# Spreading the row-2 joining of a Winograd convolution over three steps of the vector engine's order

## The chip, the cores and the metric

The kernel runs on one core of one Trainium2 chip. The metric is the device time of one execution in microseconds; the runs shown for the kernel before are three, with a median of 3211.7 us (3210.56 to 3212.76). A profile is one more execution, recorded instruction by instruction. In it PE is the matrix engine, PEld its weight loads, DVE the vector engine, ACT the scalar engine, POOL and SP the other two; all five run their own instruction lists in order and wait for each other through semaphores.

## The reference

Four images of 256 channels and 64 x 64 points, in float32, pass four residual layers. Each layer is `x = x + layer(groupnorm(x))`.

```python
# layer 0: 3x3 convolution, group norm, relu, non-local attention over all 4096 points
xs = conv_general_dilated(x, smooth_w, (1, 1), 'SAME') + smooth_b
xs = relu(group_norm(xs, gn1_w, gn1_b))
f = einsum('bnc,bcm->bnm', theta_x, phi_x)      # theta, phi, g: 1x1 convolutions of xs, 128 channels
y = einsum('bnm,bmc->bnc', softmax(f), g_x)
layer0 = group_norm(conv1x1(y, w_w, w_b)) * 0.1 + xs
# layer 1: linear attention (4 heads of 32) between two rms norms
# layer 2: per-image 3x3 depthwise and 256x256 pointwise kernels, made from pooled features
# layer 3: a softmax mixture of four 256x256 matrices applied to every point
```

The change concerns the 3x3 convolution of layer 0 alone.

## The kernel before, in words

**Images and rounds.** The four images go one after another through layer 0's attention, which is PE's largest work. Image 0's convolution runs alone at the start (`convolve_first`). Then come rounds b = 0, 1, 2: while PE does the attention of image b (`attend`, line 604 on), the engines also do layers 1 to 3 of image b - 1 (`tail`; in round 0 only a weight scaling) and then the convolution of image b + 1 (`convolve`, line 472). A last round has no convolution.

**What sets the order.** The order on all engines is the order in which the Python code issues instructions (a manual schedule). The round's side work is a `Chain`, a generator that yields a cost in steps; a rate (1.5 in round 0, 0.86 in rounds 1 and 2) turns costs into steps of the attention. One attention step issues a block of logits (`pf`, line 620), its exponentials on ACT into `pr` (line 621), the products `py` of the block before (line 659) and DVE's addition of that block to the running sum `tot`. Between steps, `Chain.tick` runs what was put off by `w.later(n, f)`: f runs after n ticks.

**The convolution.** It is a Winograd scheme that makes 4 x 2 output points from tiles of 6 x 4 input points, 128 channels to a half, two halves. `a` counts the six input rows of a tile and `k` the four columns, in the order 1, 2, 0, 3. For each row a, DVE forms the row combination `ra` (with the helper `rt`) from the normalised image `xp` in `down` (line 329 on); these operations yield 0.35 each. Then for each k DVE forms `v` (`across`), and one tick later PE multiplies v with the filters `u` (`products`, line 377; four f32 products of 128 x 512, each two passes of PE, into two PSUM banks). For k = 1 ACT copies the banks to `one`; for the others DVE joins the banks one tick later into the row's result `dst` (`joined`, line 388).

**The joining of rows.** The results of rows 0, 1, 3 go directly into the output image `big`, at rows 0, 1, 3 of each group of four. Those of rows 2, 4, 5 go to a temporary `t` of the pool `k4` or are added. When row 2 is complete (k = 3), output rows 0, 1 and 2 are formed from it, for each of the two output halves `oh`, by the three operations of `joining` (line 426):

```python
return [(tt, y2, y1, t, ALU.add), (tt, y1, y1, t, ALU.subtract), (tt, y0, y0, y2, ALU.add)]
```

Each is one tensor_tensor of 128 x 1024 on DVE. In the kernel before, `join` puts both halves off by one tick, so all six stand together in DVE's list. Row 4, which has twelve such operations, goes another way: they are put in the list `rest`, and `some(3)` takes three of them at each of four ticks.

**Buffers.** `k4` holds ten tiles of 128 x 1024 that v, t, pr, tot and others share; `bank` holds PSUM's eight banks of 128 x 512, shared by all matrix products.

Of the kernel before, what the change touches and what calls it, by code (L numbers as in the profile page):

```python
# [14 lines left out]
NH = 2  # L15
# [66 lines left out]
def conv_preact_fast(ctx: ExitStack, tc: tile.TileContext, guard, x, wc, wtpg, ww, wqkv, wout, w1cat, wd2,  # L82
# [187 lines left out]
    def stats_tile():  # L270
        return sp.tile([P, NH, 8, 6], F32, name="st")
# [65 lines left out]
    def down(a, to, prior=None):  # L337

        A, T = inside(to), rt
        mul, add, sub = ALU.mult, ALU.add, ALU.subtract  # L340
        if a in (0, 5):
            lo = 0 if a == 0 else 1
            return [(stt, o, i, f, j, mul, add) for h in range(NH) for o, i, f, j in (
                (A[:, h], rows_of(lo + 2, h), -5.0, rows_of(lo + 4, h)), (A[:, h], rows_of(lo, h), 4.0, A[:, h]))]
        if a == 1:
            return [(stt, o[:, h], rows_of(k, h), -4.0, rows_of(k + 2, h), mul, add)
                    for h in range(NH) for o, k in ((A, 2), (T, 1))] + [(tt, A[:, h], A[:, h], T[:, h], add) for h in range(NH)]
        if a == 3:
            return [(tt, o[:, h], rows_of(k + 2, h), rows_of(k, h), sub) for h in range(NH) for o, k in ((A, 2), (T, 1))] + [
                (stt, A[:, h], T[:, h], 2.0, A[:, h], mul, add) for h in range(NH)]  # L350
        return [(stt, A[:, h], T[:, h], -2.0 if a == 2 else -4.0, inside(prior)[:, h], mul, add) for h in range(NH)]

    def across(k, rows):

        def col(j):
            return rows[:, :, :, j:j + MX * (IX - 1) + 1:MX]

        v = k4("v")
        first, second, op = ((0, 2, ALU.subtract), (1, 2, ALU.add), (2, 1, ALU.subtract), (1, 3, ALU.subtract))[k]
        tt(v.rearrange("p (h y x) -> p h y x", h=NH, x=IX), col(first), col(second), op)  # L360
        return v
# [78 lines left out]
    def input_stats():  # L440

        st = stats_tile()
        for h in range(NH):
            for c in range(8):
                nc.vector.bn_stats(st[:, h, c, :], xin[:, h, bass.ts(c, RB), :].rearrange("p y x -> p (y x)"))
                yield 0.3
        return (yield from group_finish(st, avg8, 1e-5))

    def normalise(gm, rstd):
        nb = negated(gm, rstd)  # L450
        for q in range(4):
            rows = bass.ts(q, HW // 4)
            nc.vector.tensor_scalar(xin[:, 0, rows, :], xin[:, 0, rows, :], gm[:, 0:1], rstd[:, 0:1],
                                    ALU.subtract, ALU.mult)
            nc.scalar.activation(xin[:, 1, rows, :], xin[:, 1, rows, :], AF.Identity,
                                 bias=nb[:, 1:2], scale=rstd[:, 1:2])
            yield 0.5

    def copy_x(b):
        for h in range(NH):  # L460
            nc.sync.dma_start(out=xs_d[b, h], in_=x[b, bass.ts(h, P), :])

    def normed_relu(w, b, st):

        bias = vec_s[:, V_SB, :]
        _, gm, rstd = yield from group_finish(st, avg32, 1e-5, bias)
        sc, sh = affine(gm, rstd, vec_s[:, V_G1W, :], vec_s[:, V_G1B, :], bias, 1.0)
        for c in range(N // CH):
            cols = bass.ts(c, CH)
            for h in range(NH):  # L470
                nc.scalar.activation(big[:, h, cols], big[:, h, cols], AF.Relu, bias=sh[:, h:h + 1], scale=sc[:, h:h + 1])  # L471
                w.later(1, lambda h=h, cols=cols: add_by_dma(xs_d[b, h, :, cols], big[:, h, cols]))
                yield 0.3

    def convolve(w, b):

        _, gm, rstd = yield from input_stats()
        yield from normalise(gm, rstd)
        st = stats_tile()
        products, joined, _, rows_joined, joining, stats = joiner(st)  # L480
        PRODUCTS = [(a, k) for a in range(TY) for k in ACROSS]

        rest = []

        def some(n):
            for _ in range(min(n, len(rest))):
                op, *args = rest.pop(0)
                op(*args)

        def multiply(a, k, v, u):  # L490
            ps = products(a, k, v, u)
            if k != 1:
                w.later(1, lambda: join(a, k, ps))

        def join(a, k, ps):
            dst = joined(a, k, ps)
            if k == 3 and a == 4:

                for oh in range(NH):
                    rest.extend(joining(a, oh, dst[oh]))  # L500
                for j in range(4):
                    w.later(1 + j, lambda: some(3))
                for j in range(3):
                    w.later(5 + j, lambda j=j: stats(j))
            elif k == 3:
                some(len(rest))
                for oh in range(NH):
                    w.later(1, lambda oh=oh: rows_joined(a, oh, dst[oh]))

        def load_filters(i):  # L510
            res = []
            for oh in range(NH):
                u = wk.tile([P, NH, P], F32, tag="u", name="u", bufs=4)
                nc.sync.dma_start(out=u, in_=filters[PRODUCTS[i][0], oh, :, PRODUCTS[i][1]])
                res.append(u)
            return lambda oh, h: res[oh][:, h, :]

        us = load_filters(0)
        copy_x(b)
        for i, (a, k) in enumerate(PRODUCTS):  # L520
            if k == 1:
                for op, *args in down(a, ra, ra):
                    op(*args)
                    yield 0.35
            v, u = across(k, ra), us
            if i + 1 < len(PRODUCTS):
                us = load_filters(i + 1)
            w.later(1, lambda a=a, k=k, v=v, u=u: multiply(a, k, v, u))
            yield 0.8
        yield from w.pending()  # L530
        stats(3)
        yield from normed_relu(w, b, st)
# [1196 lines left out]
```

## Time and profile before

| what | value |
|---|---|
| median of three runs | 3211.7 us |
| profiled execution, its own time | 3210.14 us |
| its span, first to last instruction | 3208.4 us |
| mean granted PE clock | 0.986 |
| PE busy | 3071.0 us (96%) |
| DVE busy | 2075.8 us (65%) |
| ACT busy | 1146.0 us (36%) |
| instructions | 24196 |
| DVE: row-2 and other additions of t into big, 128 x 1024 | 30, mean 1221 ns |
| DVE: v, 128 x 1024 | 72, mean 1220 ns |
| PE: 128 x 512 products of the convolution | 576 here, mean 599 ns |

Busy times overlap, and PE's matmuls are pipelined: a record of 592 ns starts about 430 ns after the one before. A wait row reads: who waited, for whom, us in total, times, longest. A timeline row reads: start, duration (of the group), engine, line, operation, output and inputs, shape, count, and in brackets the idle time ahead of it with its releaser. A row of the windows view has the stretch and its length, then for each engine the busy time and the number of instructions, then the PE clock granted, the share of the DMA engines and GB/s.

### The profile page before, as it was taken

The numbers are of one execution on the slowest core, as the hardware profiler recorded it, in microseconds if no ns is written. First come the engines' busy times: TensorE is split into PE (matmuls) and PEld (weight loads), VectorE is DVE, ScalarE is ACT, GpSimd is POOL, SyncE is SP. The second block draws the span as 40 slices with busy tenths as digits, with TensorE's granted clock in tenths as the row PEclk, the third lists the DMA queues.
The fourth block names the chain that finished last, engine by engine and source line by source line (L and its number), as shares of the span: only waits on it lengthen the run. The fifth ranks groups of instructions, "written<-read, shape, count | busy, mean of one in ns | idle before, by whom it ended". The sixth has DMA issues, their size and how long they took to land.

```text
span 3208.4 us, 24196 instructions
## 1 busy us (share of the span) xinstructions
PE 3071.0 (96%) x8494; PEld 1476.7 (46%) x8494; DVE 2075.8 (65%) x2603; ACT 1146.0 (36%) x2139; POOL 129.4 (4%) x169
## 2 busy tenths in 40 slices
PE   6899999999999999999999999999999999996797
PEld 3354444445564444444565444444555534443533
DVE  8636776443556986876537796878353768855575
ACT  2133224333555332223364432312355443333520
POOL 0000000000010000000011000000000100000100
PEclk9999999999999999999999999999999999998998
DMA  5510113001100023113200102210510010121101
GB/s 180 173 39 27 33 34 62 7 13 63 49 10 27 13 72 118 40 33 76 101 11 6 35 20 90 101 38 27 129 42 1 10 40 7 49 70 46 50 0 73
DMA packets 73792, 161.66 MB, mean 50 GB/s; under 512 B 7744, under 2 KB 39232, under 8 KB 70720
## 3 DMA queue, kind: packets, MB, share of 16 engines
q1 hardware_dynamic: 69056, 143.27, 13.1%
q0 software_dynamic: 4608, 16.78, 2.9%
q8 instruction: 69, 1.13, 0.2%
q14 instruction: 59, 0.48, 0.0%
HBM read 103.40 MB, written 73.40 MB: 55 GB/s over the span
## 4 chain that ended last, share of the span: by engine, by line
PE 79%; DVE 12%; issue 5%; ACT 2%; DMA 0%; POOL 0%; SPq 0%; POOLq 0%; ACTq 0%
PE pf L620 23%; PE py L659 23%; PE ps_conv L382 8%; PE ps_qkv L748 5%; DVE dw L112 4%; PE ps_tp L596 3%; PE ps_ex L1059 3%; PE ps_pw L922 2%; DVE tot L109 2%; PE ps_g L601 2%; PE ps_h L881 2%; PE ps_wy L643 2%; PE ps_o L813 1%; PE ps_ctx L768 1%; PE ps_ss L735 1%
## 5 line engine op out<-in xcount | busy, mean ns | idle before, releaser
L621 ACT ACTIVATE pr<-pf 128x512 f32<-128x512 f32 x1024 | 604.1, 596 | 1227.7 <-PE pf L620 1203.7
L620 PE MATMUL pf<-tpg 128*128 128x512 f32 x2048 | 968.7, 595 | 1.4 <-ACT pr L621 1.4
L659 PE MATMUL py<-pr,tpg 128*128 128x512 f32 x2048 | 962.1, 592 | 3.0 <-ACT pr L621 2.9
L109 DVE TENSOR_TENSOR tot<-tot,pr 128x1024 f32<-128x1024 f32 x448 | 546.5, 1220 | 263.3 <-ACT pr L621 261.7
L659 PEld LDWEIGHTS py<-pr,tpg 128*128 128x128 f32 x2048 | 388.8, 190 | 494.2 <-issue 478.3
L620 PEld LDWEIGHTS pf<-tpg 128*128 128x128 f32 x2048 | 381.6, 190 | 447.3 <-issue 419.2
L112 DVE SCALAR_TENSOR_TENSOR dw<-xp,dk,dw 128x1008 f32<-128x1008 f32 x224 | 283.1, 1268 | 7.0 <-ACT dw L914 3.7
L382 PE MATMUL ps_conv<-v,u 128*128 128x512 f32 x576 | 260.7, 599 | 12.7 <-issue 9.0
L382 PEld LDWEIGHTS ps_conv<-v,u 128*128 128x128 f32 x576 | 110.3, 192 | 154.0 <-issue 147.0
L748 PE MATMUL ps_qkv<-wqkv_s,xg 128*128 128x384 f32 x384 | 130.7, 490 | 0.0
L596 PE MATMUL ps_tp<-big,wtpg_s 128*128 128x512 f32 x256 | 116.8, 599 | 3.0 <-ACT big L471 3.0
L189 POOL TENSOR_TENSOR rstd<-rstd,half 128x2 f32<-128x2 f32 x24 | 16.8, 701 | 2478.8 <-DVE rstd L294 2285.2
L109 DVE TENSOR_TENSOR tpg<-ps_g,bg_s 128x512 f32<-128x512 f32 x32 | 22.1, 692 | 144.3 <-PE ps_g L601 144.3
L922 PE MATMUL ps_pw<-dw,pk 128*128 128x512 f32 x224 | 103.8, 597 | 10.9 <-DVE dw L112 10.9
L634 DVE RECIPROCAL inv<-pss 128x512 f32<-128x512 f32 x32 | 107.2, 3351 | 7.3 <-PE pss L632 7.3
L748 PEld LDWEIGHTS ps_qkv<-wqkv_s,xg 128*128 128x128 f32 x384 | 72.2, 190 | 52.5 <-issue 8.9
L756 DVE TENSOR_REDUCE qs<-qk 128x16 f32<-128x512 f32 x24 | 16.5, 686 | 123.4 <-ACT qk L750 123.4
L109 DVE TENSOR_TENSOR v<-ra 128x1024 f32<-128x1024 f32 x72 | 86.7, 1220 | 0.4
L597 ACT ACTIVATE tpg<-ps_tp,btp_s 128x512 f32<-128x512 f32 x64 | 43.7, 686 | 118.4 <-PE ps_tp L596 118.4
L922 PEld LDWEIGHTS ps_pw<-dw,pk 128*128 128x128 f32 x224 | 42.7, 191 | 65.4 <-issue 50.9
L596 PEld LDWEIGHTS ps_tp<-big,wtpg_s 128*128 128x128 f32 x256 | 47.5, 193 | 54.3 <-issue 49.8
L750 ACT ACTIVATE qk<-ps_qkv,rinv 128x256 f32<-128x256 f32 x96 | 45.4, 473 | 74.2 <-PE ps_qkv L748 71.2
(273 smaller groups left out, 2948.2 us busy)
## 6 DMA issues: line engine op xcount, KB each, us to landing
u<-filters SPq DMA_DIRECT2D x144, 128.0 KB, 2.3
xp<-in_x_dram SPq DMA_DIRECT2D x16, 1024.0 KB, 6.4
xs_d<-big POOLq DMA_DIRECT2D x32, 512.0 KB, 11.3
wy_d<-wt SPq DMA_DIRECT2D x32, 512.0 KB, 3.0
out_dram<-res SPq DMA_DIRECT2D x64, 256.0 KB, 2.0
wy<-wy_d SPq DMA_DIRECT2D x28, 512.0 KB, 5.1
xs<-xs_d SPq DMA_DIRECT2D x24, 512.0 KB, 5.3
wp<-in_wp_dram SPq DMA_DIRECT2D x16, 512.0 KB, 4.6
```

Source lines behind the costliest of these rows:

```text
L109: nc.vector.tensor_tensor(o, a, b, op)
L112: nc.vector.scalar_tensor_tensor(o, a, s, b, op0, op1)
L382: nc.tensor.matmul(ps[oh], u(oh, h), v[:, bass.ts(h, 512)], start=(h == 0), stop=(h == NH - 1))
L596: nc.tensor.matmul(ps, wtpg_s[:, h, k, :], big[:, h, cols], start=(h == 0), stop=(h == NH - 1))
L601: nc.tensor.matmul(ps[:, j, :], big[:, h, bass.ts(4 * c + j, P)], wtpg_s[:, h, 2, :], start=(h == 0), stop=(h == NH - 1))
L620: nc.tensor.matmul(pf, phi[:, bass.ts(2 * m + s, P)], theta[:, bass.ts(q, 512)], start=True, stop=True)
L621: nc.scalar.activation(pr[:, bass.ts(s, 512)], pf, AF.Exp)
L634: nc.vector.reciprocal(inv, pss)
L659: nc.tensor.matmul(py, g[:, bass.ts(2 * m + s, P)], probs[i][:, bass.ts(s, 512)], start=(m == 0 and s == 0), stop=(m == NM - 1 and s == 1))
L748: nc.tensor.matmul(ps[:, 0:3 * HID], xg[:, h, bass.ts(j, P)], wqkv_s[:, h, :], start=(h == 0), stop=(h == NH - 1))
L922: nc.tensor.matmul(ps, pk[:, h * NH * P + oh * P:h * NH * P + (oh + 1) * P], dw[h][:, bass.ts(s, 512)], start=(h == 0), stop=(h == NH - 1))
L1059: nc.tensor.matmul(ps, wm[h][:, bass.ts(oh, P)], big[:, h, cols], start=(h == 0), stop=(h == NH - 1))
```

## The change

In `join`, row 2 gets a case of its own. Its six operations go to the list `rest`, half 0's three first, and two of them are taken at each of the next three ticks. Rows 3 and 5 keep the old way, row 4 its own.

```diff
@@ -502,6 +502,11 @@
                     w.later(1 + j, lambda: some(3))
                 for j in range(3):
                     w.later(5 + j, lambda j=j: stats(j))
+            elif k == 3 and a == 2:
+                for oh in range(NH):
+                    rest.extend(joining(a, oh, dst[oh]))
+                for j in range(3):
+                    w.later(1 + j, lambda: some(2))
             elif k == 3:
                 some(len(rest))
                 for oh in range(NH):
```

`some(n)` takes up to n operations off the front of `rest` and issues them. In the built program the lists of PE, ACT, POOL and SP stand as before. On DVE the order changes at three places, one in each round with a convolution. With J1 to J6 for the six operations, ra and rt for row 3's input combination:

```
round 0 before: tot J1 J2 J3 J4 J5 J6 ra rt tot ra ra tot v tot v
round 0 after:  tot J1 J2 ra rt tot J3 J4 ra ra tot J5 J6 v tot v
rounds 1, 2 before: tot J1 J2 J3 J4 J5 J6 ra v tot v v tot v tot
rounds 1, 2 after:  tot J1 J2 ra v tot J3 J4 v v tot J5 J6 v tot
```

## The prediction

> **What bounds the kernel now.** I read the page's shares first, then its chain, then PE's waits, then the timeline of the one place that the diff touches.
>
> ```profile
> PE 3071.0 (96%) x8494; PEld 1476.7 (46%) x8494; DVE 2075.8 (65%) x2603; ACT 1146.0 (36%) x2139; POOL 129.4 (4%) x169
> PE 79%; DVE 12%; issue 5%; ACT 2%; DMA 0%; POOL 0%; SPq 0%; POOLq 0%; ACTq 0%
> PE ps_conv L382 <- issue: 9.0, 2, 4.5
> PE ps_conv L382 <- DVE v L109: 3.7, 2, 2.0
> ```
>
> PE is busy 96% of the span, so a DVE edit pays only where PE stands still for DVE. The last two lines (PE's waits) say that the convolution's products stood 9.0 us in two waits, longest 4.5, put down to "issue", and 3.7 us in two waits for v. The timeline of the round that convolves image 2 shows the first of the two 4.5:
>
> ```profile
> 1373.00 1.22 DVE L109 TENSOR_TENSOR tot<-tot,pr 128x1024 f32<-128x1024 f32 x1
> 1374.13 2.48 DVE L109 TENSOR_TENSOR big<-big,t 128x1024 f32<-128x1024 f32 x2
> 1376.53 1.22 DVE L109 TENSOR_TENSOR big<-big 128x1024 f32<-128x1024 f32 x1
> 1377.37 1.88 PE L659 MATMUL py<-pr,tpg 128*128 128x512 f32 x4
> 1377.66 2.48 DVE L109 TENSOR_TENSOR big<-big,t 128x1024 f32<-128x1024 f32 x2
> 1380.06 1.22 DVE L109 TENSOR_TENSOR big<-big 128x1024 f32<-128x1024 f32 x1
> 1381.19 1.22 DVE L112 SCALAR_TENSOR_TENSOR ra<-rt,ra 128x1024 f32<-128x1024 f32 x1
> 1382.44 1.23 DVE L109 TENSOR_TENSOR v<-ra 128x1024 f32<-128x1024 f32 x1
> 1383.77 5.37 PE L382 MATMUL ps_conv<-v,u 128*128 128x512 f32 x8 [4.52 <-issue]
> 1388.97 1.88 PE L620 MATMUL pf<-tpg 128*128 128x512 f32 x4
> ```
>
> The six joining operations of row 2 are the four DVE lines with big. Behind them stand row 3's last input operation (ra) and its first v; v ends at 1383.67 and the products start 0.10 later. So "issue" is this wait for v: it was held on a separate wait instruction in PE's queue, which this line of the products' source view shows as long as 8932 ns, from 1374.8 (hence to 1383.7):
>
> ```profile
> L382 PEldq EVENT_SEMAPHORE  x4: 51/51/8932, 1374.8 to 1391.5; - x4
> ```
>
> The eight matmuls then take 5.20 us to the next group, where the same eight take 3.43 later (1402.71 to 1406.14). The windows view has the clock: 0.90 over 17 us is half speed for 3.4 us.
>
> ```profile
> 1373.00:1390.00 17.00, 12.48 (x26) 5.24 (x25) 16.25 (x15) 3.56 (x6) 0.00 (x0) 0.90 0.02 8
> 2131.00:2148.00 17.00, 12.48 (x26) 5.12 (x25) 16.02 (x14) 3.75 (x7) 0.00 (x0) 0.90 0.02 8
> ```
>
> The round of image 3 is the same picture (second row): the joining at 2131.91, products at 2141.55 after 4.52 idle, next group 5.21 later. The round of image 1 is milder:
>
> ```profile
> 393.35 1.22 DVE L109 TENSOR_TENSOR v<-ra 128x1024 f32<-128x1024 f32 x1
> 394.62 3.70 PE L382 MATMUL ps_conv<-v,u 128*128 128x512 f32 x8 [2.03 <-DVE v L109]
> ```
>
> [...] both 4.52 us pauses were followed by 3.4 us at half, the 2.03 us one was not. [...] the trace has 1220, and independent ones start 1.13 apart. [...] here v waits behind the joining on DVE and PE's later groups behind the products.
>
> **The change part by part.** Nothing is added or removed: PE, ACT, POOL and SP keep their order, DMA issues included; on DVE six operations in each of three rounds move. Against the profiled execution (3210.14 us, span 3208.4):
>
> Round of image 2. New order: tot, J1, J2, ra, v, tot, J3, J4, v, v, tot, J5, J6, v. J1 starts at 1374.13 as before. The pair costs 2.40 (1374.13 to 1376.53), so ra starts at 1376.53, v 1.25 later (as 1381.19 to 1382.44) at 1377.78, ends at 1379.01, and PE may start at 1379.11. PE is free of its py group at 1377.37 + 4 x 0.43 = 1379.09. The products start at 1379.11 in place of 1383.77: 4.66. Without the pause I take the clock to stay full, 3.43 in place of 5.20: 1.77. Together 6.43.
>
> Round of image 3. J1 2131.91, ra 2134.31, v 2135.56 to 2136.79, products 2136.89 in place of 2141.55: 4.66; 5.21 becomes 3.43: 1.78. Together 6.44.
>
> Round of image 1. The chain ticks more often against the input operations, so all six still stand ahead of v: J1, J2, ra, rt, tot, J3, J4, ra, ra, tot, J5, J6, v. Before, the 12 operations from 379.47 took 13.88, with two pairs that cost 2.40 where free ones cost 2.27 (a wait for the operation just ahead). Now only the first pair pays it: v comes 0.13 earlier. The pause stays at 1.9.
>
> Sum 6.43 + 6.44 + 0.13 = 13.0: profiled time 3197.1. The runs shown have their median 1.6 above the profiled execution, at 3211.7; so 3198.7.
>
> **What the four deferred operations delay.** They cost nothing if DVE's later work still comes in time. For image 2, all of PE's times 6.43 earlier: after v, DVE runs tot 1378.92, J3 1380.05, J4 1381.19, v of k=2 1382.32 to 1383.55 (PE needs it at 1392.41 - 6.43 = 1385.98: 2.4 to spare, the narrowest), v of k=0 until 1384.7 (needed at 1389.4), tot, J5 1385.73, J6, v of k=3 1388.0 to 1389.2 (needed at 1396.28), tot, then the joining of k=2 from 1390.3 to 1392.7 and of k=0 to 1393.7. These free PSUM banks of the pool of 8: py, four for k=2 and k=0, two for logits make seven, k=3's first bank is the eighth, its second (1398.0) and the next logits (1406.14 - 6.43 = 1399.7) need freed ones: 5.3 and 6.0 to spare. Row 4's v, after two ra, ends at 1397.5 and is needed at 1403.15. The cover is DVE's idle time: 2.17 + 1.58 + 0.43 + 0.43 + 1.03 + 0.92 before 1407 on the old timeline, 6.6 us, which PE's new start eats. The tots, which free probabilities, come earlier (1378.92 for 1383.59, 1384.6 for 1386.99). Head 1's t stays in the k4 pool until J5, some 5 us longer; buffers rotate differently, and row 4's first v now also waits for a wy_d write, issued at 1321.53 with a median of 2.7 us to land: long done.
>
> **The rivals.** (1) The pause goes but the clock's half-speed stretches do not all: 13.0 less one or two of 1.77 is 9.5 to 11.2, so 3200.5 to 3202.2. For it: [...] the windows view has the clock at 0.99 between 780 and 935, though PE is busy 151.79 of those 155 us. Against: with v on time PE has no pause here. (2) PE stands for something other than v, and nothing changes: 3211.7. The word "issue" speaks for it; the 0.10 us from v's end in both rounds and the round of image 1, where the same wait is named v, speak against. (3) Partial debt: DVE is up to 3 us later than worked out, past the 2.4 us margin of v for k=2, and PE stops again there: 1 to 5 us back over two rounds, 3200 to 3204. (4) Slower: the same backlog decides at the PSUM banks. Each us that the joining of k=2 comes beyond the 5.3 us margin is a us of PE. To end 0.2% (6.4 us) above before, each round must give back 6.43 and lose 3.2 more, so the joining must come 15 us later than 1392.7, that is thirteen more 1.13 us operations ahead of it; only four are moved there. Time 3218 if it were so. I see no such work in the order.
>
> **How the numbers follow.** The main case has 0.76, with its own range 3196.5 to 3201.0: the runs shown spread by 2.2, and half-speed stretches elsewhere (the tail's clock is 0.92) may fall differently by one or two of 1.77. Rival 1 has 0.09, rival 3 0.06, rival 2 0.05, rival 4 0.04. The range 3195.5 (two such stretches fewer) to 3204.0 takes in the main case and rivals 1 and 3. A difference of 0.2% (6.4 us) is about what measurement can tell from none: main, rival 1 and most of 3 are faster, 0.90; same 0.06; slower 0.04.
>
> **What would show it.** In the changed kernel's PE waits, the "issue" row of ps_conv is gone or below 0.5 us and v's row stays near 3.6; the timeline has the products of row 3 in the second and third rounds start within 0.2 us of the py group's end, and the clock is 1.00 over those 17 us; the first round keeps a pause of about 1.9; DVE's busy time stays 2075.8 within 1. Wrong would be: a new wait of PE within 30 us after, on v or big, or the two pauses still there.

## The result, and the profile after

The changed kernel takes 3198.27 us (median of four runs, 3196.53 to 3198.95) against 3212.09 us for the kernel before (four runs, 3210.56 to 3212.76). The ratio is 0.9957, with a 95% interval of 0.994 to 0.9974. That is 13.8 us, where 13.0 was forecast; the time forecast was 3198.7. The profiled execution took 3198.95 us with a span of 3197.2, 11.2 less than before.

First the shares of the page, and three rows of PE's waits, of the changed kernel. Line numbers above 505 are five higher than before.

```profile
PE 3069.2 (96%) x8494; PEld 1476.0 (46%) x8494; DVE 2074.2 (65%) x2603; ACT 1146.1 (36%) x2139; POOL 129.2 (4%) x169
```

```profile
PE ps_row L414 <- DVE ra L112: 6.8, 1, 6.8
PE ps_conv L382 <- DVE v L109: 3.5, 2, 1.9
PE ps_tp L601 <- ACT big L471: 3.0, 1, 3.0
```

The work is the same: as many matmuls, as many DVE instructions. The row "ps_conv <- issue", 9.0 us in two waits, is gone, and the row for v is nearly what it was, 3.5 us for 3.7. The timeline of the round that convolves image 2 shows how:

```profile
1374.63 1.22 DVE L109 TENSOR_TENSOR tot<-tot,pr 128x1024 f32<-128x1024 f32 x1
1375.76 2.48 DVE L109 TENSOR_TENSOR big<-big,t 128x1024 f32<-128x1024 f32 x2
1378.15 1.22 DVE L112 SCALAR_TENSOR_TENSOR ra<-rt,ra 128x1024 f32<-128x1024 f32 x1
1378.99 1.88 PE L664 MATMUL py<-pr,tpg 128*128 128x512 f32 x4
1379.40 1.23 DVE L109 TENSOR_TENSOR v<-ra 128x1024 f32<-128x1024 f32 x1
1380.73 3.67 PE L382 MATMUL ps_conv<-v,u 128*128 128x512 f32 x8
1383.95 2.36 DVE L109 TENSOR_TENSOR v<-ra 128x1024 f32<-128x1024 f32 x2
1384.24 1.88 PE L625 MATMUL pf<-tpg 128*128 128x512 f32 x4
1387.67 7.03 PE L382 MATMUL ps_conv<-v,u 128*128 128x512 f32 x16
```

Two joining operations instead of six stand ahead of ra. v ends at 1380.63, and the products start at 1380.73, straight behind the py group (1378.99 + 4 x 0.43 = 1380.71). The products are four, and each shows as two matmul records. The next group follows 3.51 us later, not 5.20: the clock stayed at 1.00. The windows view says the same of both rounds (PEclk is the third number from the end):

```profile
1373.00:1390.00 17.00, 17.00 (x41) 7.50 (x40) 16.93 (x16) 4.76 (x8) 0.00 (x0) 1.00 0.05 15
2124.00:2142.00 18.00, 18.00 (x43) 7.81 (x42) 17.93 (x16) 5.04 (x9) 0.00 (x0) 1.00 0.06 16
```

PE is busy all of the 17 us, where it was busy 12.48 before. Measured from the tot ahead of the joining to the logits behind the first products, the round of image 2 took 15.97 before (1373.00 to 1388.97) and 9.61 now (1374.63 to 1384.24): 6.36 less. The round of image 3 went from 15.98 (2130.78 to 2146.76) to 9.62 (2125.98 to 2135.60): again 6.36. Both were forecast at 6.4. In the round of image 1 the pause stays, but in this execution the clock falls behind it, to 0.86 on the mean from 390 to 402 us, where it was 1.00 before:

```profile
392.50 1.88 PE L664 MATMUL py<-pr,tpg 128*128 128x512 f32 x4
396.28 5.40 PE L382 MATMUL ps_conv<-v,u 128*128 128x512 f32 x8 [1.90 <-DVE v L109]
401.51 1.02 PE L625 MATMUL pf<-tpg 128*128 128x512 f32 x2
```

The products to the next group take 5.23 us instead of 3.53 before.

### The profile page after: what moved, and what is told of

Read it like the earlier page. It is cut to its first block, busy times and chain, and to the rows that moved or that the text cites. A ratio compares the mean times of both kernels' runs of the same rounds, so it can differ in the third digit from the quotient of the medians.

```text
span 3197.2 us, 24194 instructions
## 1 busy us (share of the span) xinstructions
PE 3069.2 (96%) x8494; PEld 1476.0 (46%) x8494; DVE 2074.2 (65%) x2603; ACT 1146.1 (36%) x2139; POOL 129.2 (4%) x169
## 3 DMA queue, kind: packets, MB, share of 16 engines
q8 instruction: 69, 1.13, 0.2%
## 4 chain that ended last, share of the span: by engine, by line
PE 79%; DVE 12%; issue 5%; ACT 2%; DMA 0%; POOL 0%; SPq 0%; POOLq 0%; ACTq 0%
PE pf L625 23%; PE py L664 23%; PE ps_conv L382 8%; PE ps_qkv L753 5%; DVE dw L112 4%; PE ps_tp L601 4%; PE ps_ex L1064 3%; PE ps_pw L927 3%; DVE tot L109 2%; PE ps_g L606 2%; PE ps_h L886 2%; PE ps_wy L648 2%; PE ps_o L818 1%; PE ps_ctx L773 1%; PE ps_ss L740 1%
## 5 line engine op out<-in xcount | busy, mean ns | idle before, releaser
L820 ACT ACTIVATE junk<-ps_o 128x256 f32<-128x256 f32 x128 | 49.2, 384 | 63.5 <-PE ps_o L818 60.5
```

## The experiments

The theory was that a joining operation costs PE time only where it stands ahead of row 3's first v. Rivals: that taking two at a time is itself what helps; that the deferred work is paid for later; that DVE, at 65%, has room everywhere. In each group of runs the kernel before ran beside them on the same chip: 3211.09 us for the first four, 3211.19 for the others. The two agree within 0.1 us, so runs of both groups are set side by side.

**One round alone.** First the round of image 1 alone, then that of image 3 alone.

```diff
-            elif k == 3 and a == 2:
+            elif k == 3 and a == 2 and b == 1:
```

> The new place of the six operations in the round of image 1 alone; the rounds of images 2 and 3 as before. Theory (only operations that stand ahead of row 3's first v cost PE time): all six stay ahead of that v in this round, so PE's pause there goes from 2.03 to 1.9 us and the other two rounds keep 4.52 each; within 2 us of the kernel before. Rival (two at a time is itself what helps, wherever it is): a third of the gain, 4 us or more faster.

Measured: 3211.16 us, ratio 1.0 (0.9992 to 1.0009). The pause in that round is 1.90 us, the other two stay at 4.52:

```profile
PE ps_conv L382 <- issue: 9.0, 2, 4.5
...
PE ps_conv L382 <- DVE v L109: 3.6, 2, 1.9
```

Spreading the six operations in a round where they all stay ahead of v is worth nothing that can be measured. The rival of this run falls.

```diff
-            elif k == 3 and a == 2:
+            elif k == 3 and a == 2 and b == 3:
```

> The new place in the round of image 3 alone. Theory: that round's pause of 4.52 us and the half clock after it go, the others stay; 6.4 us faster than before (5 to 8.5). Rival (the gain comes from somewhere else, such as the other use of the buffers): not half of the whole change's gain.

Measured: 3204.21 us, ratio 0.9979 (0.9971 to 0.9986), so 6.9 us less: half of the change's gain. One of the two 4.52 us pauses is left, in the round of image 2, with half clock after it (5.21 us to the next group), and the round of image 3 shows none:

```profile
PE ps_conv L382 <- issue: 4.5, 1, 4.5
```

Image 2's round was not run alone. Twice 6.9 is 13.8 us, and the change gained 13.8 in its first measurement and 12.6 in its second, so the rounds add up as far as the scatter lets one see.

**How many stand ahead of v.**

```diff
-                    w.later(1 + j, lambda: some(2))
+                    w.later(1 + j, lambda n=(4, 1, 1)[j]: some(n))
```

> Four operations at the first step, then one and one: in the rounds of images 2 and 3 two more of the 1.13 us operations stand ahead of v than in the change. Theory: a pause of 2 x 1.13 = 2.3 us (2.0 to 2.4) in place of none in each of these two rounds, followed by half clock in some of them; 4.0 to 8 us slower than the change, still 5 to 9 us faster than before. Rival (spreading over steps is what helps): as fast as the change.

Measured: 3204.12 us, ratio 0.998 (0.9971 to 0.9988), so 5.5 us slower than the change (3198.61 in its second measurement, below). The timeline of the round of image 2:

```profile
1376.01 1.22 DVE L109 TENSOR_TENSOR big<-big 128x1024 f32<-128x1024 f32 x1
1377.15 1.22 DVE L109 TENSOR_TENSOR big<-big,t 128x1024 f32<-128x1024 f32 x1
1378.28 1.22 DVE L112 SCALAR_TENSOR_TENSOR ra<-rt,ra 128x1024 f32<-128x1024 f32 x1
1379.54 1.23 DVE L109 TENSOR_TENSOR v<-ra 128x1024 f32<-128x1024 f32 x1
```

```profile
1376.86 1.88 PE L664 MATMUL py<-pr,tpg 128*128 128x512 f32 x4
1380.87 3.67 PE L382 MATMUL ps_conv<-v,u 128*128 128x512 f32 x8 [2.13 <-issue]
```

The two added operations (the first two lines) hold v back, and PE pauses 2.13 us in both rounds. So six, four and two operations ahead give pauses of 4.52, 2.13 and none: 1.1 to 1.2 us for each, the time that it takes in DVE's order: in the trace of before, operations of this size last 1.22 us each, start 1.13 apart where they are independent, and a pair whose second waits for its first took 2.40. The two pauses are 4.3 of the 5.5 us. The work is spread over three steps here too, and that does not help.

**One lump, but behind v.** All six together, one tick later than before.

```diff
-                for j in range(3):
-                    w.later(1 + j, lambda: some(2))
+                for j in range(1):
+                    w.later(2, lambda: some(6))
```

> All six in one lump, as before, but one tick later than before, so in the rounds of images 2 and 3 they stand right behind row 3's first v and the addition after it; in the round of image 1 still ahead of v. Theory (position, not the spread, decides): no pause for this v in the two rounds; the lump ends just in time for the v of k=2, at most 0.3 us late; within 1.5 us of the change. Rival (the lump itself stops PE, wherever it is): pauses of 2 us or more at k=2, and the gain is half or less.

Measured: 3199.12 us, ratio 0.9963 (0.995 to 0.9977), the change's time within the scatter. The lump now stands between v and the two v of k = 2 and 0:

```profile
1376.10 1.23 DVE L109 TENSOR_TENSOR v<-ra 128x1024 f32<-128x1024 f32 x1
...
1378.37 2.48 DVE L109 TENSOR_TENSOR big<-big,t 128x1024 f32<-128x1024 f32 x2
1379.80 3.60 PE L382 MATMUL ps_conv<-v,u 128*128 128x512 f32 x8
1380.77 1.22 DVE L109 TENSOR_TENSOR big<-big 128x1024 f32<-128x1024 f32 x1
1381.90 2.48 DVE L109 TENSOR_TENSOR big<-big,t 128x1024 f32<-128x1024 f32 x2
1384.30 1.22 DVE L109 TENSOR_TENSOR big<-big 128x1024 f32<-128x1024 f32 x1
...
1385.43 2.35 DVE L109 TENSOR_TENSOR v<-ra 128x1024 f32<-128x1024 f32 x2
1386.71 4.56 PE L382 MATMUL ps_conv<-v,u 128*128 128x512 f32 x10
```

The first v of the pair ends at about 1386.66 and PE starts on it at 1386.71, without a pause: just in time. So the gain needs no spreading, only another place.

**The change again, and its margin.** The change was measured again, with the next three runs on the same chip.

> The change itself, on the chip of the three runs beside it, so that they can be compared with it. 11 to 14.5 us faster than before; PE's pauses of 4.52 us gone in the rounds of images 2 and 3; the pause of 1.9 us in the round of image 1 there, with half clock after it or not.

Measured: 3198.61 us, ratio 0.996 (0.9946 to 0.9973); 12.6 us less than before. The 1.90 us pause of image 1's round was again followed by half clock (0.86 on the mean from 390 to 402 us, as in the change's first profile).

To test the margin of 2.4 us that the forecast worked out for the v of k = 2, four additions of the same size were put behind J4 in the rounds of images 2 and 3.

```diff
-                for j in range(3):
-                    w.later(1 + j, lambda: some(2))
+                rest[4:4] = [(tt, dst[0], image[:, 1, :, 0, :], image[:, 1, :, 0, :], ALU.add)] * (4 if b > 1 else 0)
+                for j in range(3): w.later(1 + j, lambda n=(2, 4+2 if b > 1 else 2, 2)[j]: some(n))
```

> The change with four more additions of 128 x 1024 on DVE behind J4 in the rounds of images 2 and 3 (they write the temporary t of half 0 when it is no longer read). Theory (the deferred work has 2.4 us to spare before PE's k=2 products, and what exceeds it is paid one for one): 4 x 1.13 = 4.5 us more DVE work gives a pause of 2.1 us (1.9 to 2.4) ahead of the k=2 products in both rounds; 4 to 8 us slower than the change. Rival (DVE is only 65% busy, so it has room everywhere): no pause, within 1.5 us of the change. Rival of the other side (there was no margin): pauses of 4.5 us.

Measured: 3204.5 us, ratio 0.9978 (0.997 to 0.9986), 5.9 us slower than the change.

```profile
1383.38 4.99 DVE L109 TENSOR_TENSOR t<-big 128x1024 f32<-128x1024 f32 x4
...
1388.30 2.35 DVE L109 TENSOR_TENSOR v<-ra 128x1024 f32<-128x1024 f32 x2
1389.57 7.13 PE L382 MATMUL ps_conv<-v,u 128*128 128x512 f32 x16 [2.30 <-DVE v L109]
```

The four took 4.92 us of DVE's order (1383.38 to 1388.30; they start 1.23 apart, and all write the same tile, where independent operations of this size start 1.13 apart), and PE paused 2.30 us in each round. So 4.92 - 2.30 = 2.6 us was the room, against 2.4 forecast. The forecast counted from start to start; so counted, PE stood 2.47 us (1385.38 + 4 x 0.43 = 1387.10 to 1389.57), and the room is 2.45. Beyond it the added time of DVE came out as PE's time, at an engine that is busy 65% of the span. The two pauses are 4.6 of the 5.9 us; in the second round half clock followed as well (0.86 on the mean from 2140 to 2152 us).

**The deferred operations left out.** This kernel leaves out J3 to J6 in the rounds of images 2 and 3.

```diff
-                for j in range(3):
-                    w.later(1 + j, lambda: some(2))
+                del rest[2 if b > 1 else 6:]
+                for j in range(3): w.later(1 + j, lambda: some(2))
```

> The four operations that the change defers (J3 to J6) are left out in the rounds of images 2 and 3, so part of row 2's joining is not computed there. Theory (where the change puts them they cost PE nothing): within 1.5 us of the change. Rival (they still cost something downstream, in the PSUM banks or in later rows): 2 us or more faster than the change.

Measured: 3197.62 us, ratio 0.9958 (0.9945 to 0.9972), 1.0 us below the change, with overlapping runs (3197.08 to 3198.79 against 3196.74 to 3199.16). So eight operations of 1.13 us, 9 us of DVE work, cost PE no more than the scatter. PE's pauses in the rounds are those of the change. The deferred work fills time in which DVE would stand idle: from 1373 to 1400 us DVE works 22.16 us here and 26.90 in the change, and PE is busy all of these 27 us in both.

**One tick later.** The first experiment points to what is left: in the round of image 1 all six are still ahead of v. Each pair was put off by one tick more.

```diff
-                    w.later(1 + j, lambda: some(2))
+                    w.later(2 + j, lambda: some(2))
```

> The change with each pair one tick later. In the rounds of images 2 and 3 v was in time already: nothing. In the round of image 1 two of the six now stand behind row 3's first v, so v comes 2 x 1.13 = 2.3 us earlier and the pause of 1.9 us goes, with the half clock that follows it in some executions. Theory: 1.5 to 3.8 us faster than the change. Rival (that pause is paid back by a later wait, such as the 1.65 us one ahead of row 5): within 0.8 us of the change, the later pause longer.

Measured: 3193.95 us (3193.3 to 3199.16), ratio 0.995 (0.9937 to 0.9964): 4.7 us below the change's median and the fastest of all; four of its five runs lie below every run of the change. The gain is larger than the 1.5 to 3.8 us expected. PE's waits for v in the rounds, and the round of image 1:

```profile
PE ps_conv L382 <- DVE v L109: 1.7, 1, 1.7
```

```profile
390.49 1.88 PE L664 MATMUL py<-pr,tpg 128*128 128x512 f32 x4
390.73 1.22 DVE L109 TENSOR_TENSOR v<-ra 128x1024 f32<-128x1024 f32 x1
392.20 3.60 PE L382 MATMUL ps_conv<-v,u 128*128 128x512 f32 x8
393.00 1.21 DVE L109 TENSOR_TENSOR big<-big,t 128x1024 f32<-128x1024 f32 x1
```

The pause of 1.90 is gone and row 5's, 1.66 us, is unchanged, so nothing is paid back there. Against the profile of the change's second measurement, the group behind image 1's first products starts 5.50 us earlier (395.64 for 401.14). Of these, 1.63 were there already at 158 us (156.87 for 158.50), ahead of anything that the edit touches. The other 3.87 are the edit's: 2.07 for the pause, counted from start to start, and 1.80 for the half clock behind it. So in the profiles the edit's own gain is about the top of what was expected. The rest of the 4.7 is not shown to come from the edit; the start, where these two profiles differ by 1.63, is a guess at its place.

## Why the prediction was right, and where it was off

**What PE waited for.** The reading that "issue" in the wait row was v holds: with v early the row is gone, and with v 2.3 us later (four ahead) it is back at 4.3 us in two waits. Rival 2 falls.

**The sum.** Forecast 6.43 + 6.44 + 0.13, from the trace of before alone. Measured 6.36 + 6.36 + 0.13 (the pause went from 2.03 to 1.90). In a round, the pause gave 4.67 us where 4.66 was forecast and the clock 1.69 where 1.77 was. The term that was off is the time of the products without a pause: 3.51 in place of 3.43 us. The 3.43 was taken from products whose v had long been ready, and in the trials in which row 3's first v is earlier still (the lump behind v, one tick later) these products do take 3.43; in the change v comes just in time. The times of DVE's order came out to the hundredth: v starts 3.64 us behind J1 where 3.65 was worked out (1377.78 less 1374.13), the v of k = 2 at 8.19 behind J1 in both.

**The deferred work.** "2.4 to spare, the narrowest" was measured as 2.6, and the four deferred operations as free within the scatter. So the backlog of rivals 3 and 4 is not reached by the four operations that the change defers. Rival 3's mechanism is real: it was seen with four operations more, 2.30 us of pause in each round, and would start with the third by an estimate from the room of 2.6 us and the 1.23 of each. Rival 4's, the PSUM banks, was met by no run.

**The clock.** Here the forecast was incomplete. It took the half clock away in the two rounds, an estimate from the three pauses of the trace of before, and the clock was 1.00 there in the changed kernel's profile. It left image 1's pause at 1.9 with no half clock behind it, as in the trace of before, and in the changed kernel's profiled execution that pause did cost 1.70 more (5.23 for 3.53). In the same execution a stretch of half clock near 834, which the kernel before shows behind a pause of 1.11 us and eight small matmuls, is absent. The windows view from 825 to 845, before and then after:

```profile
825.00:845.00 20.00, 18.89 (x59) 9.89 (x57) 6.29 (x15) 11.22 (x20) 1.76 (x3) 0.91 0.00 0
```

```profile
825.00:845.00 20.00, 18.89 (x57) 9.38 (x56) 9.50 (x20) 11.19 (x19) 1.76 (x3) 1.00 0.00 0
```

Put together for the profiled executions: row 3's first ra of image 1 stands 1.79 us later than before (377.86 for 376.07), a delay from the start of the kernel, where a stretch of half clock ends at 157.6 in place of 155.2; image 1's products add 1.57; the stretch at 834 takes 1.70 back; the two rounds take 6.36 each; the sum is -11.06, and the spans differ by 11.2. So the profiled pair alone would have shown less than the forecast, mostly for a reason that the edit doesn't touch, and the medians, 13.8 and 12.6 apart in the two measurements, lie around it. One stretch of half clock more or less is 1.7 us, so that 13.8 came within 0.8 of 13.0 is in part luck. Rival 1 was wrong of the two rounds, where the half clock went with the pause, and right in kind elsewhere: single stretches come and go from execution to execution. The last section has what the traces show of it.

**One sign was too tight.** DVE's busy time was to stay within 1 us and fell by 1.6, with as many instructions. Nothing of the argument rests on it.

## What to carry to other kernels

In every round shown here DVE's operations started in the order of its list, and one of them cost PE time only where it stood ahead of something for which PE was waiting: six, four and two ahead of v went with pauses of 4.52, 2.13 and 0 us, six behind it with none. Look for the consumer's pause first, and count the operations that stand ahead of the awaited one and could stand behind it. Moving them behind it was free here up to the slack of the next awaited operation, which the timeline of before gave to within 0.2 us; beyond it the price was about one for one (4.92 us of added work, 2.6 of room, 2.30 of pause), at an engine that was busy 65% of the span. A chain that yields at another rate in another round puts the same edit at another place, so look at every round in the built order. And a pause of PE can cost more than its length: taking away the 4.52 us pauses here gave 6.36 us each, 1.69 of it from the half clock that had followed.

## What was not expected

The clock fell behind pauses of about 2 us too, where the forecast had counted half clock behind those of 4.52 alone. In the ten executions profiled here (before, the change twice, seven other kernels), pauses of PE of 1.9 to 2.3 us ahead of row 3's products occurred 13 times, and half clock followed 3 of them; the 4.52 us pauses occurred 5 times, and it followed all 5. Each stretch was 3.4 us and cost about 1.7. In the change it came behind the 1.90 us pause both times, while the trial in image 1's round alone, with the same pause of 1.90 in the same place, had none.

What differs is how the pause lies against the times at which the clock changes. The traces of before and of the change have 11 and 9 stretches of half clock. In each of the two, all stretches start whole multiples of 3.413 us apart, to within 0.002 us, and each lasts a whole multiple of it, save the last, which the end of the kernel cuts off. Steps of 3.413 us, counted from these starts, lie elsewhere against the kernel's start in each execution: the first stretch starts at 141.51 us before and at 143.93 in the change. Here are the two steps at image 1's pause, first of the change and then of the trial in image 1's round alone (PE's busy time is the second number behind the stretch, its clock the third from the end):

```profile
393.11:396.52 3.41, 1.51 (x4) 0.45 (x4) 3.41 (x4) 0.19 (x1) 0.00 (x0) 1.00 0.00 0
396.52:399.93 3.41, 3.41 (x5) 1.35 (x5) 3.41 (x4) 0.03 (x1) 0.00 (x0) 0.50 0.00 0
```

```profile
390.07:393.48 3.41, 1.99 (x5) 0.57 (x3) 3.41 (x4) 0.65 (x2) 0.00 (x0) 1.00 0.00 0
393.48:396.89 3.41, 2.92 (x7) 1.44 (x8) 3.41 (x4) 0.59 (x1) 0.00 (x0) 1.00 0.00 0
```

In the change the whole pause lies in one step, and the next step runs at half clock. In the trial the same pause is cut into 1.42 and 0.49 us, and the clock stays. In the trace of before the 2.03 us pause is cut into 1.51 and 0.52, and the clock stays too; its two 4.52 us pauses each leave 3.2 us of one step idle, and half clock follows. This does not explain every case: in the trials two other short pauses left 1.91 and 1.98 us of one step idle, and no half clock followed. So these executions do not give an idle time from which on the clock falls.

The stretch near 834 goes the same way. Its pause of 1.11 us and the eight matmuls of 128 x 1 behind it take 2.0 us. Before, they lie within one step (831.00 to 834.42), and half clock starts at its end. In the change the end of a step at 836.84 cuts them (835.14 to 837.16), and the clock stays at 1.00. No run set where the steps lie. That a pause of 1.90 us lies whole in one step would happen in 1.5 of 3.41 positions, an estimate from these two lengths that takes all positions as equally likely. So it is no wonder that half clock followed in both executions of the change, and image 1's pause has no fixed price.
